# Chunk and residual loads issued from ScalarE's queue, and new lengths in a hand-written planner, in a convolution, attention and expert kernel

## The chip, the cores and the metric

The kernel runs on one core of a Trainium2 chip. A core has a matrix engine (TensorE, PE in the profile), a vector engine (VectorE, DVE), an activation engine (ScalarE, ACT), a general engine (GpSimd, POOL) and a queue engine (SyncE, SP) that issues transfers. Each works through its own list of instructions in order; semaphores order them between engines. The metric is the device time of one execution in microseconds (us); less is better.

## The reference

Input x is 8 images of 56 x 56 tokens with 128 channels, float32. In short:

```python
# layer 0: deformable convolution block
xp = x @ w_in + b_in
h = gelu(batchnorm(depthwise_conv3x3(x)))
offset = h @ w_off + b_off                    # 4 groups x 9 points x 2
mask = softmax(h @ w_msk + b_msk)             # over the 9 points
y = sum over points of mask * bilinear(xp, offset)
x = x + gamma1 * layer_norm(y @ w_out + b_out)
x = x + gamma2 * layer_norm(gelu(x @ w_fc1 + b_fc1) @ w_fc2 + b_fc2)
# layer 1: t = tokens of x, 3136 for each image
n = layer_norm(t)
t = t + softmax(causal((n @ Wq) @ (n @ Wk).T / sqrt(3136))) @ (n @ Wv)
n = layer_norm(t)
probs = softmax(n @ gate_w.T + gate_b, over the tokens)
# each of 64 experts takes its 8 best tokens of an image, pools them,
# runs gelu(. @ weight1) @ weight2, and adds the result back to them
t = t + scatter_add(...)
```

## The kernel before

All images go through one scheduled stage, then the experts' weights are streamed and the output is assembled (lines from 1050 on). An image is cut into 4 groups, three of 896 tokens and one of 448, so there are 32 groups. Seven generator functions each do one step for one group: `prepare` loads chunks of 448 tokens (xin), transposes them (ptx), copies them into a padded tile (xg), keeps a shifted copy for the residual (xc, stored to DRAM as xTd), and writes the projected image to DRAM (img). `plan` makes the 3x3 convolution (h), offsets and mask, and 25 tap weights a token (taps). `sample` gathers for each tile of 128 tokens 25 neighbours from DRAM (g, lines 471 to 496), multiplies them by the taps on VectorE (L484) and sums them on GpSimd (L489 to L496) into ys. `project` loads the residual (xT), transposes ys (pty), multiplies by w_out (py), normalises and adds (pta), runs the two layers (ph, hid, pm), normalises and adds again (ptb) and transposes back into t. `largest` makes the keys (zT), queries (qT) and the largest score of each query (sc, mx); `attend` makes scores again (st), exponentials (pe) and the weighted sum (av); `after` adds, normalises, makes the gate's logits (lg) and its best tokens (cv).

The groups are pipelined by a planner that runs when the kernel is built. Every generator yields `need(engine, us, ...)` ahead of each step: the engine that it takes, how long it is taken to last, whether it takes or gives one of the rotating PSUM buffers ("gen" 2, "sc" 3) or gather buffers ("g" 3), and from when its inputs are there (`since`). The planner keeps a time at which each engine is free and repeatedly advances the generator whose next step has the smallest start plus a lag for its place in the pipeline:

```python
min(able, key=lambda l: l.start() + BEHIND * (l.at + l.lag)).step()
```

The instructions are emitted in that order, so it fixes the order of every engine's list. The lengths only decide the order; at run time the semaphores decide the times. Nothing else hangs on the planner's times.

Loads are issued by SyncE in the order of emission. `bring` issues the load of a chunk, two chunks ahead; its tile has two buffers, so it waits until the transposes (L317) have read the chunk before the last one. `project` issues both residual loads of a group at its beginning (L557); that tile, too, has two buffers. The gathers (L479) are issued by SyncE, three to four transfers for a tile, and wait for one of three buffers. Stores of xTd, img, t2d and logd are issued by ScalarE.

Of the kernel before, what the change touches and what calls it, by code (L numbers as in the profile page):

```python
# [16 lines left out]
P = 128  # L17
C = 128
# [53 lines left out]
def local_kernel(ctx, tc, a, out, flag):  # L72
# [221 lines left out]

    xins = {}

    def bring(b, c, at):

        b, c = b + c // NCHUNK, c % NCHUNK
        if b < NB and (b, c) not in xins:  # L300
            xin = wk.tile([TP, 4, C], F32, tag="xin", name=f"xin{b}_{c}", bufs=2)
            nc.sync.dma_start(
                xin, x[b, c * CH : (c + 1) * CH, :].rearrange("(t p) d -> p t d", p=TP)
            )
            xins[b, c] = xin, at + 6.0

    def prepare(b, s):
        im = imgs[b % 2].rearrange("(h w) c -> h w c", w=IW)
        for c in range(2 * s, min(2 * s + 2, NCHUNK)):
            r = CHR * (c % 2)  # L310
            bring(b, c, 0.0)
            bring(b, c + 1, 0.0)
            xin, there = xins.pop((b, c))
            at = yield need(PE, 0.45, take="gen", since=there)
            pt = gen(f"ptx{b}_{c}")
            for i in range(4):
                nc.tensor.transpose(pt[:, i * TP : (i + 1) * TP], xin[:, i, :], ident[:TP, :TP])  # L317
            bring(b, c + 2, at)
            yield need(ACT, 2.0, give="gen")
            p3 = pt[:, :CH].rearrange("c (h w) -> c h w", w=HW)  # L320
            xg = rows_tile(b, s)
            nc.scalar.copy(xg[:, 1 + r : 1 + r + CHR, 1 : HW + 1], p3)
            xc = wk.tile([C, CH], F32, tag="xc", name=f"xc{b}_{c}")
            nc.scalar.activation(xc, pt[:, :CH], AF.Identity, bias=shift)
            nc.scalar.dma_start(xTd[b % 2][:, c * CH : (c + 1) * CH], xc)
            if r == 0 and c > 0:
                nc.scalar.copy(rows_tile(b, s - 1)[:, XROWS - 1, 1 : HW + 1], p3[:, 0])
            if r and c + 1 < NCHUNK:
                nc.scalar.copy(rows_tile(b, s + 1)[:, 0, 1 : HW + 1], p3[:, CHR - 1])
            yield need(PE, 0.95, take="gen")  # L330
            pq = gen(f"pq{b}_{c}")
            xf = xg.rearrange("c h w -> c (h w)")
            for i in range(4):

                f0 = (1 + r + 2 * i) * PW + 1
                nc.tensor.matmul(
                    pq[:W2, i * C : (i + 1) * C], xf[:, f0 : f0 + W2], w_in, start=True, stop=True
                )
            yield need(DVE, 0.7, give="gen")
            st = wk.tile([W2, 4, C], F32, tag="st", name=f"st{b}_{c}", bufs=2)  # L340
            nc.vector.tensor_add(
                st,
                pq[:W2, :].rearrange("p (t c) -> p t c", t=4),
                b_in.unsqueeze(1).to_broadcast([W2, 4, C]),
            )
            yield need(ACT, 0.8)
            for r in range(2):
                dst = im[2 + CHR * c + r : 2 + CHR * c + r + CHR - 1 : 2, 2 : HW + 2, :]
                nc.scalar.dma_start(dst.rearrange("t x c -> x t c"), st[r * PW : r * PW + HW])
# [4 lines left out]
    def plan(b, s):  # L354
# [3 lines left out]
        h = wk.tile([C, GT * P], F32, tag="h", name=f"h{b}_{s}")  # L358
        h3 = h[:, :N].rearrange("c (h w) -> c h w", w=HW)
        for k in range(NP):  # L360
            yield need(DVE, 0.15 + 0.0012 * N) if k else need(ACT, 0.2 + 0.001 * N)
            dy, dx = divmod(k, 3)
            src = xg[:, dy : dy + nr, dx : dx + HW]
            if k == 0:
                nc.scalar.activation(h3, src, AF.Copy, scale=dw[:, :1])  # L365
            else:
                nc.vector.scalar_tensor_tensor(  # L367
                    h3, src, dw[:, k : k + 1], h3, op0=ALU.mult, op1=ALU.add
                )
# [164 lines left out]
    def transposed(o, z, i0, m, n, name):  # L534
# [6 lines left out]
        yield need(ACT, 0.15 + 0.00085 * n, give="gen")  # L541
        nc.scalar.copy(o, pt[:, :n])

    def project(b, s):
        nm = f"{b}_{s}"
        nt, N = tiles(s), tokens(s)
# [2 lines left out]
        rest[b, s] = t  # L549
        if N < nt * P:  # L550
            nc.gpsimd.memset(t[:, nt - 1], 0.0)
        xTs = []
        for i0, m in banks(nt):
            n = min(m * P, N - i0 * P)
            r0 = (GT * s + i0) * P
            xT = wk.tile([C, 4 * P], F32, tag="xT", name=f"xT{nm}_{i0}", bufs=2)
            nc.sync.dma_start(xT[:, :n], xTd[b % 2][:, r0 : r0 + n])  # L557
            xTs.append(xT)
        for i0, m in banks(nt):
            n = min(m * P, N - i0 * P)  # L560
            xT = xTs.pop(0)
            yT = wk.tile([C, 4 * P], F32, tag="yT", name=f"yT{nm}_{i0}")
            if n < m * P:
                nc.gpsimd.memset(yT[:, n : m * P], 0.0)
            yield from transposed(yT[:, :n], ys, i0, m, n, f"y{nm}_{i0}")
            yield need(PE, 0.3 + 0.23 * m)
            py = ps.tile([P, 512], F32, tag="held", name=f"py{nm}_{i0}")
            nc.tensor.matmul(py[:, : m * C], three, b_out[:, : m * C], start=True, stop=False)
            for i in range(m):
                nc.tensor.matmul(  # L570
                    four(py, m)[:, i, :],
                    yT[:, i * P : (i + 1) * P],
                    w_out,
                    start=False,
                    stop=i == m - 1,
                )
            yield from add_normed(xT[:, :n], four(py, m), 0, f"a{nm}_{i0}")
            hid = wk.tile([P, 4, 4 * P], F32, tag="hid", name=f"hid{nm}_{i0}")
            if n < m * P:
                nc.gpsimd.memset(hid[:, :, n : m * P], 0.0)  # L580
            for f in range(4):
                there = yield need(PE, 0.0018 * n, take="gen", since=there if f else None)
                ph = gen(f"ph{nm}_{i0}_{f}")
                nc.tensor.matmul(  # L584
                    ph[:, :n], fc1[:, f * P : (f + 1) * P], xT[:, :n], start=True, stop=True
                )
                yield need(ACT, 0.15 + 0.00105 * n, give="gen", kind=GELU)
                nc.scalar.activation(  # L588
                    hid[:, f, :n], ph[:, :n], AF.Gelu, bias=b_fc1[:, f : f + 1]
                )  # L590
            yield need(PE, 0.3 + 0.92 * m)
            pm = ps.tile([P, 512], F32, tag="held", name=f"pm{nm}_{i0}")
            nc.tensor.matmul(pm[:, : m * C], three, b_fc2[:, : m * C], start=True, stop=False)
            for i in range(m):
                for f in range(4):
                    nc.tensor.matmul(  # L596
                        four(pm, m)[:, i, :],
                        hid[:, f, i * P : (i + 1) * P],
                        fc2[:, f, :],
                        start=False,  # L600
                        stop=i == m - 1 and f == 3,
                    )
            yield from add_normed(xT[:, :n], four(pm, m), 1, f"b{nm}_{i0}")

            yield need(PE, 0.12 * m, take="gen")
            pt = gen(f"pt2{nm}_{i0}")
            for i in range(m):
                w = min(P, n - i * P)
                nc.tensor.transpose(
                    pt[:w, i * C : (i + 1) * C], xT[:, i * P : i * P + w], ident  # L610
                )
            yield need(ACT, 0.6, give="gen")
            full = n // P
            nc.scalar.copy(t[:, i0 : i0 + full], four(pt, full))
            if full < m:
                nc.scalar.copy(t[: n % P, nt - 1], pt[: n % P, full * C : m * C])


    def moments(t, nt, name):
# [320 lines left out]
    free = {PE: 0.0, DVE: 0.0, ACT: 0.0, POOL: 0.0}  # L940
    rings = {"gen": [0.0] * 2, "sc": [0.0] * 3, "g": [0.0] * GB}
    table = [None]
    BEHIND = 1.0

    class Line:


        def __init__(self, make, lag, ready, source):
            self.make, self.ready, self.source, self.lag = make, ready, source, lag
            self.at, self.now, self.next, self.time, self.ended = 0, None, None, 0.0, {}  # L950

        def able(self):

# [7 lines left out]
                self.next = next(self.now)  # L961
            return not self.next.take or bool(rings[self.next.take])

        def start(self):
            n = self.next
            at = self.time if n.since is None else n.since
            if n.take:
                at = max(at, min(rings[n.take]) + (8.0 if n.take == "g" else 0.0))
            return max(at, free[n.engine])

        def step(self):
# [4 lines left out]
            if n.kind and n.kind != table[0]:  # L976
                table[0] = n.kind
                at += 1.3
            at += n.us
            free[n.engine] = at  # L980
            if n.give:
                rings[n.give].append(at)
            self.time = at + 0.1
            try:
                self.next = self.now.send(self.time)
            except StopIteration:
# [45 lines left out]
    while True:  # L1032
        able = [lines[o] for o in order if lines[o].able()]
        if not able:
            break
        min(able, key=lambda l: l.start() + BEHIND * (l.at + l.lag)).step()
    assert all(l.at == len(groups) for l in lines.values())


# [914 lines left out]
```

## Time and profile before

| | |
|---|---|
| median of 3 runs | 4209.79 us (4205.06 to 4210.52) |
| the profiled execution | 4213.55 us, its span 4211.7 us |
| TensorE's mean granted clock | 0.841 of full speed |
| DMA | 467.32 MB, mean 111 GB/s |
| SyncE's dynamic queue, q1 | 388.06 MB |
| ScalarE's dynamic queue, q10 | 74.60 MB |
| 0 to 3850 us: PE, DVE, ACT, POOL busy | 2914.50, 2513.91, 1676.36, 1946.31 us |
| 3850 to 4212 us: PE, DVE, ACT, POOL busy | 319.65, 75.51, 19.71, 1.24 us |

The span is the time from the first to the last instruction of the profiled execution; its device time is a little longer. Busy time of an engine counts what it computes, not the issuing of transfers and not its waits. "SPq" and "ACTq" are the queues in which SyncE and ScalarE wait and issue. A wait names the waiting engine, tile and line, then what it waited for: "PE ph L584 <- DVE xT L532" is TensorE waiting to start ph until VectorE has written xT. The chain of waits is followed back from the last instruction; it says which work the end hung on.

### The profile page before, as it was taken

What the parts mean: (1) busy time and instruction counts of PE and PEld (TensorE: products, weight loads), DVE (VectorE), ACT (ScalarE), POOL (GpSimd) and SP (SyncE); (2) the same over time, 40 slices, a digit from 0 to 9 for tenths busy, and PEclk for the clock granted to TensorE, in tenths of its full rate; (3) what the DMA queues carried; (4) which work ended last, traced back from release to release, by engine and by line L of the source; (5) the groups of instructions that cost most, each with busy time, mean ns of one, the idle gap of its engine ahead of it and who ended that gap; (6) DMA issues with size and microseconds to landing.
All of it is one profiled execution on the core that took longest, in us unless ns stands there. A gap on an engine that the chain in (4) does not pass through costs nothing.

```text
span 4211.7 us, 38352 instructions
## 1 busy us (share of the span) xinstructions
PE 3234.1 (77%) x12403; PEld 1980.6 (47%) x12403; DVE 2589.4 (61%) x4152; ACT 1696.1 (40%) x3738; POOL 1947.5 (46%) x1785
## 2 busy tenths in 40 slices
PE   3268589688875898588866988688848896996998
PEld 2134345344442444344443545444524453454987
DVE  5753676678665876577667776676757765531014
ACT  2133334444453544354453545444635453342000
POOL 1554555465445555554555545654565555201000
PEclk8578699889987999799987999899979997996555
DMA  5565444455444454544454455554454455003548
GB/s 150 113 131 112 98 112 109 102 118 121 99 100 104 106 111 96 122 107 111 100 122 95 108 110 111 119 115 107 105 121 103 109 112 113 15 11 103 155 135 247
DMA packets 333088, 467.32 MB, mean 111 GB/s; under 512 B 21080, under 2 KB 192908, under 8 KB 332364
## 3 DMA queue, kind: packets, MB, share of 16 engines
q1 hardware_dynamic: 209068, 388.06, 41.1%
q10 hardware_dynamic: 122784, 74.60, 6.6%
q0 software_dynamic: 1024, 2.10, 0.2%
q8 instruction: 100, 1.64, 0.2%
q14 instruction: 112, 0.92, 0.1%
HBM read 403.20 MB, written 61.49 MB: 110 GB/s over the span
## 4 chain that ended last, share of the span: by engine, by line
PE 36%; DVE 19%; POOL 11%; ACT 4%; issue 3%; DMA 3%; SPq 0%; DVEq 0%; ACTq 0%; POOLq 0%
PE sc L694 7%; DVE g L484 6%; PE av L778 6%; PE st L758 6%; POOL g L489 4%; PE epo L1097 3%; PE eph L1079 3%; POOL g L491 2%; PE ph L584 2%; DVE h L367 2%; PE pf L1130 2%; DVE taps L447 1%; PE pm L596 1%; DVE mx L709 1%; DMA g<-img 1%
## 5 line engine op out<-in xcount | busy, mean ns | idle before, releaser
L489 POOL TENSOR_TENSOR g<-g 128x1536 f32<-128x1536 f32 (+1 forms) x200 | 701.9, 3510 | 978.1 <-DVE g L484 874.2
L778 PE MATMUL av<-pe,zk 128*128 128x448 f32 (+6 forms) x1600 | 717.3, 539 | 92.7 <-ACT pe L771 82.3
L484 DVE TENSOR_TENSOR g<-g,tp 128x3200 f32<-128x3200 f32 (+1 forms) x200 | 694.7, 3478 | 44.8 <-ACT tp L467 16.8
L758 PE MATMUL st<-qT,zT 128*128 128x448 f32 (+6 forms) x1600 | 698.8, 527 | 3.8 <-ACT qT L729 1.3
L694 PE MATMUL sc<-zT,qT 128*128 128x512 f32 (+6 forms) x1600 | 650.7, 537 | 52.7 <-DVE mx L709 46.2
L709 DVE TENSOR_REDUCE mx<-sc 128x1 f32<-128x512 f32 (+6 forms) x800 | 451.3, 586 | 316.0 <-PE sc L694 268.2
L771 ACT ACTIVATE pe<-st 128x448 f32<-128x448 f32 (+6 forms) x800 | 393.5, 504 | 456.6 <-PE st L758 343.6
L778 PEld LDWEIGHTS av<-pe,zk 128*128 128x128 f32 (+1 forms) x1600 | 286.7, 200 | 317.6 <-issue 145.1
L694 PEld LDWEIGHTS sc<-zT,qT 128*128 128x128 f32 (+1 forms) x1600 | 283.7, 193 | 304.5 <-issue 130.1
L758 PEld LDWEIGHTS st<-qT,zT 128*128 128x128 f32 (+1 forms) x1600 | 300.1, 199 | 245.4 <-issue 217.7
L584 PE MATMUL ph<-xT,fc 128*128 128x512 f32 (+2 forms) x448 | 240.1, 654 | 200.6 <-DVE xT L532 178.6
L491 POOL TENSOR_TENSOR g<-g 128x768 f32<-128x768 f32 (+1 forms) x200 | 383.8, 1919 | 11.5
L367 DVE SCALAR_TENSOR_TENSOR h<-xg,dw,h 128x896 f32<-128x896 f32 (+1 forms) x256 | 356.4, 1392 | 7.4 <-ACT h L365 2.8
L584 PEld LDWEIGHTS ph<-xT,fc 128*128 128x128 f32 x448 | 91.8, 224 | 292.6 <-DVE xT L532 153.7
L596 PEld LDWEIGHTS pm<-fc,hid 128*128 128x128 f32 x1600 | 202.4, 196 | 44.3 <-issue 21.4
L596 PE MATMUL pm<-fc,hid 128*128 128x128 f32 x1600 | 214.2, 282 | 7.3 <-ACT hid L588 6.8
L493 POOL TENSOR_TENSOR g<-g 128x384 f32<-128x384 f32 (+1 forms) x200 | 212.6, 1063 | 13.3
L856 DVE MAX8 cv<-lg 64x8 f32<-64x896 f32 (+1 forms) x32 | 31.1, 972 | 278.4 <-ACT lg L843 278.4
L447 DVE TENSOR_TENSOR taps<-taps,a 128x252 f32<-128x252 f32 (+1 forms) x288 | 198.1, 688 | 1.3
L588 ACT ACTIVATE hid<-ph,b_fc 128x512 f32<-128x512 f32 (+2 forms) x224 | 138.8, 633 | 137.6 <-PE ph L584 136.0
L540 PE MATMUL pty<-ident,ys 128*128 128x128 f32 (+1 forms) x200 | 43.6, 324 | 176.9 <-POOL ys L496 171.0
L530 PE MATMUL ptb<-ident,ub 128*128 128x128 f32 (+1 forms) x200 | 50.4, 342 | 131.2 <-ACT ub L525 131.2
(238 smaller groups left out, 4979.0 us busy)
## 6 DMA issues: line engine op xcount, KB each, us to landing
g<-img SPq DMA_DIRECT2D x280, 700.0 KB
g<-img SPq DMA_DIRECT2D x56, 600.0 KB
g<-img SPq DMA_DIRECT2D x56, 500.0 KB
g<-img SPq DMA_DIRECT2D x56, 400.0 KB
g<-img SPq DMA_DIRECT2D x56, 300.0 KB
w2t<-in_L_ffn_weight_dram ACTq DMA_DIRECT2D x64, 256.0 KB
w1t<-in_L_ffn_weight_dram SPq DMA_DIRECT2D x32, 512.0 KB
xin<-in_x_dram SPq DMA_DIRECT2D x56, 224.0 KB
```

Source lines behind the costliest of these rows:

```text
L367: nc.vector.scalar_tensor_tensor(h3, src, dw[:, k : k + 1], h3, op0=ALU.mult, op1=ALU.add)
L447: nc.vector.tensor_add(dst, dst, a5[:, :nt, kx])
L484: nc.vector.tensor_mul(g3, g3, tp[:n, lt % 4].unsqueeze(2).to_broadcast([n, NTAP * NG, 32]))
L489: nc.gpsimd.tensor_add(g[:n, : 12 * C], g[:n, : 12 * C], g[:n, 12 * C : 24 * C])
L491: nc.gpsimd.tensor_add(g[:n, : 6 * C], g[:n, : 6 * C], g[:n, 6 * C : 12 * C])
L584: nc.tensor.matmul(ph[:, :n], fc1[:, f * P : (f + 1) * P], xT[:, :n], start=True, stop=True)
L596: nc.tensor.matmul(four(pm, m)[:, i, :], hid[:, f, i * P : (i + 1) * P], fc2[:, f, :], start=False, stop=i == m - 1 and f == 3,)
L694: nc.tensor.matmul(pp[:w, :n], qT[:, i * P : i * P + w], zTs[b, g][:, k0 : k0 + n], start=True, stop=not diagonal,)
L709: nc.vector.tensor_reduce(mx[:w, i, j : j + 1], pp[:w, :n], AX.X, ALU.max)
L758: nc.tensor.matmul(pp[:w, :n], zTs[b, g][:, j * P : j * P + w], qT[:, u * CH + q0 : (u + 1) * CH], start=True, stop=m <= 0,)
L771: nc.scalar.activation(pe[:w, :n], pp[:w, :n], AF.Exp, scale=SCALE)
L778: nc.tensor.matmul(av[:, q0:CH], zs[b, g][:w, j, :], pe[:w, : CH - q0], start=first, stop=last)
```

## The change

The chunk two ahead is loaded from ScalarE's queue, behind the copy that read the transposed chunk out of PSUM. The residual is loaded one bank at a time by `fetch`: from ScalarE's queue behind the copy of the bank two turns before, into the buffer that this bank has just left; the first ones, and any whose group is not yet prepared by then, from SyncE in `project`. The planner gets new lengths for the steps that now issue a load and for the convolution's taps; a factor on every length for each engine; 0.15 us between steps on different engines in place of 0.1 us behind every step; and, in the choice of the next step alone, 0.5 us more where the engine changes.

```diff
-    def bring(b, c, at):
+    def bring(b, c, at, queue):
 
         b, c = b + c // NCHUNK, c % NCHUNK
         if b < NB and (b, c) not in xins:
             xin = wk.tile([TP, 4, C], F32, tag="xin", name=f"xin{b}_{c}", bufs=2)
-            nc.sync.dma_start(
+            queue.dma_start(
                 xin, x[b, c * CH : (c + 1) * CH, :].rearrange("(t p) d -> p t d", p=TP)
             )
             xins[b, c] = xin, at + 6.0
...
-            bring(b, c, 0.0)
-            bring(b, c + 1, 0.0)
+            bring(b, c, 0.0, nc.sync)
+            bring(b, c + 1, 0.0, nc.sync)
             xin, there = xins.pop((b, c))
             at = yield need(PE, 0.45, take="gen", since=there)
             pt = gen(f"ptx{b}_{c}")
             for i in range(4):
                 nc.tensor.transpose(pt[:, i * TP : (i + 1) * TP], xin[:, i, :], ident[:TP, :TP])
-            bring(b, c + 2, at)
-            yield need(ACT, 2.0, give="gen")
+            yield need(ACT, 2.4, give="gen")
             p3 = pt[:, :CH].rearrange("c (h w) -> c h w", w=HW)
             xg = rows_tile(b, s)
             nc.scalar.copy(xg[:, 1 + r : 1 + r + CHR, 1 : HW + 1], p3)
+
+            bring(b, c + 2, at, nc.scalar)
             xc = wk.tile([C, CH], F32, tag="xc", name=f"xc{b}_{c}")
...
-            yield need(DVE, 0.15 + 0.0012 * N) if k else need(ACT, 0.2 + 0.001 * N)
+            yield need(DVE, 0.15 + 0.00139 * N) if k else need(ACT, 0.2 + 0.001 * N)
...
+    xTs = {}
+    turns = [(b, s, i0) for b in range(NB) for s in range(NGRP) for i0, _ in banks(tiles(s))]
+
+    def fetch(b, s, i0, queue):
+
+        if (b, s, i0) in xTs or not done("prepare", NGRP * b + s):
+            return
+        n = min(4 * P, tokens(s) - i0 * P)
+        r0 = (GT * s + i0) * P
+        xT = wk.tile([C, 4 * P], F32, tag="xT", name=f"xT{b}_{s}_{i0}", bufs=2)
+        queue.dma_start(xT[:, :n], xTd[b % 2][:, r0 : r0 + n])
+        xTs[b, s, i0] = xT
...
-        xTs = []
         for i0, m in banks(nt):
             n = min(m * P, N - i0 * P)
-            r0 = (GT * s + i0) * P
-            xT = wk.tile([C, 4 * P], F32, tag="xT", name=f"xT{nm}_{i0}", bufs=2)
-            nc.sync.dma_start(xT[:, :n], xTd[b % 2][:, r0 : r0 + n])
-            xTs.append(xT)
-        for i0, m in banks(nt):
-            n = min(m * P, N - i0 * P)
-            xT = xTs.pop(0)
+            fetch(b, s, i0, nc.sync)
+            xT = xTs.pop((b, s, i0))
...
-            yield need(ACT, 0.6, give="gen")
+            yield need(ACT, 1.0, give="gen")
             full = n // P
             nc.scalar.copy(t[:, i0 : i0 + full], four(pt, full))
             if full < m:
                 nc.scalar.copy(t[: n % P, nt - 1], pt[: n % P, full * C : m * C])
+
+            here = turns.index((b, s, i0)) + 2
+            if here < len(turns):
+                fetch(*turns[here], nc.scalar)
...
-    BEHIND = 1.0
+    BEHIND, SLACK = 1.0, 0.5
+    LONGER = {PE: 1.1, DVE: 1.05, ACT: 1.05, POOL: 1.05}
...
-        def start(self):
+        def start(self, slack=0.0):
             n = self.next
             at = self.time if n.since is None else n.since
+            if n.engine != self.last:
+                at += 0.15 + slack
             if n.take:
                 at = max(at, min(rings[n.take]) + (8.0 if n.take == "g" else 0.0))
             return max(at, free[n.engine])
...
-            at += n.us
+            at += n.us * LONGER[n.engine]
             free[n.engine] = at
             if n.give:
                 rings[n.give].append(at)
-            self.time = at + 0.1
+            self.time, self.last = at, n.engine
...
-        min(able, key=lambda l: l.start() + BEHIND * (l.at + l.lag)).step()
+        min(able, key=lambda l: l.start(SLACK) + BEHIND * (l.at + l.lag)).step()
```

More of the change, by code (lines that the diff above doesn't have):

```diff
@@ L949, in __init__ @@
             self.make, self.ready, self.source, self.lag = make, ready, source, lag
-            self.at, self.now, self.next, self.time, self.ended = 0, None, None, 0.0, {}
+            self.at, self.now, self.next, self.ended = 0, None, None, {}
+            self.time, self.last = 0.0, None
         def able(self):
```

## The prediction

> **What bounds the kernel now.** I read the page first: busy times, then the chain.
>
> ```profile
> span 4211.7 us, 38352 instructions
> ...
> PE 3234.1 (77%) x12403; PEld 1980.6 (47%) x12403; DVE 2589.4 (61%) x4152; ACT 1696.1 (40%) x3738; POOL 1947.5 (46%) x1785
> ...
> PE 36%; DVE 19%; POOL 11%; ACT 4%; issue 3%; DMA 3%; SPq 0%; DVEq 0%; ACTq 0%; POOLq 0%
> ```
>
> No engine is full. The chain in order of time starts at 964 us, so its shares add up to 77%, not 100%. Of what it covers, TensorE has 47%, VectorE 25%, GpSimd 14%, ScalarE 5%, transfers 4%. The work passes from engine to engine, and the time is set by how well the four in-order programs fit each other. The windows say where: 0 to 3850 us is the scheduled stage (TensorE busy 2914.50 us, VectorE 2513.91, ScalarE 1676.36, GpSimd 1946.31). The expert stage after it is untouched by the change.
>
> Next, the waits of SyncE's own queue, which issues this stage's loads (gx apart):
>
> ```profile
> SPq L479 <- POOL ys L496: 917.0, 115, 14.4
> ...
> SPq L302 <- PE ptx L317: 389.2, 22, 39.7
> SPq L479 <- DMA xTd<-xc: 274.3, 33, 17.8
> ```
>
> The columns are total us, times, longest. The first is the ordinary wait for a gather buffer. The second is a chunk load that stands at the head of the queue until TensorE has read the buffer's old chunk; gathers (L479) stand behind it. The third is a gather waiting for an older ScalarE transfer to complete.
>
> What the engines lose by that is small. In the waits of all engines, those for a transfer are far down, and those between engines lead:
>
> ```profile
> POOL g L489 <- DVE g L484: 874.2, 140, 19.4
> ...
> PE ph L584 <- DVE xT L532: 178.6, 14, 36.0
> ...
> PE pty L540 <- POOL ys L496: 171.0, 21, 15.6
> ...
> POOL g L489 <- DMA g<-img: 27.5, 5, 7.1
> ```
>
> TensorE's two waits there average 12.8 and 8.1 us, far over what one operation lasts: it arrives where the planner put it, and the other engine is late. The chain holds pieces of all three loads concerned (start, us, what):
>
> ```profile
> 1260.83 8.08 DMA xin<-in_x_dram
> ...
> 1512.74 10.24 DMA g<-img
> ...
> 2259.59 4.16 DMA xT<-xTd
> ```
>
> **Part one: SyncE's queue is freed.** By the instruction order of the two programs, 54 of 56 chunk loads and 54 of 56 residual loads go to ScalarE's queue. The chunk load is issued behind ScalarE's copy xg, which had to wait for the transposes that read the old chunk; so the wait of 389.2 us has nothing left to wait for. The residual load is issued two turns ahead, behind the copy t that waited for the buffer's last transposes. Gain: the chain's long pieces are 9.41 + 10.24 + 6.51 + 3.86 + 6.39 + 7.40 = 43.8 us of gathers, 8.1 of xin, 4.2 of xT, together 56.1 us between 964 and 3600. Scaled to a stage of 3600 us, x 3600/2636 = 77 us. That is the upper end; the lower is 0, since gathers still wait 917.0 us for GpSimd and 274.3 us and more for ScalarE's transfers. I take half, **-38 us**, because only the gathers that stood behind a chunk load gain. Where this stall goes, GpSimd's ys is late next.
>
> The Trainium skill speaks against a gain here: "DMA: Bandwidth & Descriptors", section "Issuing engines are not separate DMA queues", has transfers of all engines on the same 16 DMA engines, so that another issuing engine saves issue time alone. By it the term would be about 0; the wait of 389.2 us is issue time of that kind, and the trace decides for it.
>
> **Part two: ScalarE's new work.** The issues last 0.323 us (xin, median) and 0.368 us (xT): 54 x 0.323 + 54 x 0.368 = 37 us on ScalarE. Behind each xin issue stand xc, its store and the edge copies; behind each xT issue stands usually the next exponential pe, for which TensorE's av waits. ScalarE is idle for over half of the stage, so the lower end is its share of the chain, 5% or 2 us; the upper is 37. I take a quarter, **+9**. What waits come with them: 106 of the 108 also wait for the completion counter of an earlier transfer, often a gather. The nearest rows are ScalarE's waits for transfers before: 5.4 + 2.5 + 1.9 + 0.8 + 0.6 = 11.2 us for the 240 transfers it issues in this stage, 0.047 us each, so 5 us for 108. The far end is what SyncE pays when the other queue is late, 274.3/33 = 8.3 us each. I take **+5**, because the same engine and the same counters gave the first row; the far end becomes a rival.
>
> **Part three: the order.** This is the larger part, and it has no row of its own. Nearly every position on every engine changes. Four things can be counted.
>
> Planned against measured lengths: the lengths written into the steps before add up to 2541 us on TensorE, 2290 on VectorE, 1829 on GpSimd. In the trace these took 2914, 2514, 1946 up to 3850 us, so the plan has 0.87, 0.91, 0.94 of them. With the new lengths and factors it has 2541 x 1.1 = 2795, 2328 x 1.05 = 2444, 1829 x 1.05 = 1920, that is 0.96, 0.97, 0.99. TensorE was 4% short against VectorE and 7% against GpSimd; it is now 1% and 3% short. ScalarE was too long in the plan and stays so. Also, steps that change engines are preferred 0.5 us later, which gives producers time. The gain is bounded by TensorE's two late-partner waits, 178.6 + 171.0 = 349.6 us: at most half of it (175), and at worst none. I take a fifth, **-70**, since sums cannot say that each place improves.
>
> Table loads: the scheduled stage has 272 loads of ScalarE's function table before and 298 after (gelu against exp changes more often). Each lasts 1.283 us:
>
> ```profile
> 2439.80 1.28 ACT L771 ACT_TABLE_LOAD   x1
> 2441.09 0.98 ACT L771 ACTIVATE pe<-st 128x448 f32<-128x448 f32 x2
> 2442.09 1.28 ACT L588 ACT_TABLE_LOAD   x1
> 2443.38 0.69 ACT L588 ACTIVATE hid<-ph,b_fc 128x512 f32<-128x512 f32 x1
> ```
>
> 26 x 1.283 = 33 us; the next function starts 0.01 us behind a load, so nothing is added. ScalarE's share of the chain makes it 2, all of it 33; a quarter gives **+8**. The Trainium skill ("ScalarE: Activation LUTs", "What ACT_TABLE_LOAD costs") has a drain with each switch, about 2.66 us in all, which would make it 69 instead of 33; the rows above show no such drain.
>
> TensorE back to back: between py and its pta ScalarE squares (4 x 0.47), GpSimd takes the root (0.20 + 1.02) and ScalarE scales once (0.37), 3.5 us; with four hand-overs of 0.1 us (VectorE's multiply ended at 2222.21 us and GpSimd's add began at 2222.29) 3.9 us. In the order before, 5 of 56 py are followed at once by their pta, in the order after 21. That is 16 x 3.9 = 62 us if TensorE had other work, 0 if it had not (the planner puts nothing between where nothing is ready). A fifth: **+12**.
>
> **Small edits.** The gather's multiply, taps, attention and all arithmetic are the same and keep their durations. The xc copy starts 0.32 us later, behind the xin issue, and its store waits that much; TensorE's pq needs xg alone. Both are in part two.
>
> **Sum.** -38 + 9 + 5 - 70 + 8 + 12 = -74 us. The profiled execution took 4213.55 us (span 4211.7 and 1.85 outside), and the median of the runs is 3.76 us lower, 4209.79. 4213.55 - 74 - 3.76 = 4135.8; I forecast **4136 us**, 1.8% less.
>
> **Rivals.**
>
> *ScalarE is held by the counters* (slower). Its loads wait for gathers that SyncE can't issue yet because GpSimd hasn't freed a buffer; behind them stand pe, hid and tp, and TensorE's av waits. Against it: ScalarE lost 11.2 us on 240 such transfers. For it: SyncE lost 8.3 us at each of 33. Nine such holds (75 us) cancel the forecast's gain; one transfer in eight, 13.5 x 8.3 = 112, gives 4136 + 112 = 4248 us.
>
> *The order is worse on TensorE* (slower). The project chain stands back to back 16 times more, and no late partner comes earlier: the 70 is lost, the 12 becomes 62. 4136 + 70 + 50 = 4256 us. It decides if TensorE's waits for ua and sqa grow by more than its waits for xT and ys shrink.
>
> *The freed queue buys nothing*, since the chunk loads' place is taken by waits for ScalarE's transfers (the row of 274.3 us, grown): 4136 + 38 = 4174 us, still faster.
>
> *The order cancels out*: no late partner comes earlier, and the rest nearly cancels, 4136 + 70 = 4206 us, no change.
>
> **How the numbers follow.** A measurement of this kernel can tell about 0.2% (8 us) from no change. Chances: forecast 0.51, queue buys nothing 0.13, order cancels 0.07, ScalarE held 0.15, order worse 0.14. So faster 0.64, same 0.07, slower 0.29. The low end takes part one whole (77), a third of TensorE's late-partner waits (117), and the costs at 2 + 5 + 2 + 0: 4209.79 - 77 - 117 + 9 = 4025. The high end, 4255, takes in the held ScalarE and reaches the worse order; beyond it and below the low end I leave some 2 in 10. The two faster cases by themselves span 4025 to 4200.
>
> **What the profile after would show.** Part one is right if SyncE's wait at the chunk load is gone and its waits for ScalarE's transfers haven't grown by as much; wrong if gathers land as late as before. Part two is right if ScalarE's waits for transfers stay under 20 us. Part three is right if TensorE's waits of ph for xT and pty for ys fall together by 70 us or more, VectorE's waits for lg and pq with them, and wrong if ua, sqa or pe take their place. Table loads should number 298 in this stage. The forecast is wrong if TensorE's busy time to the end of the stage is the same and the stage doesn't end some 70 us sooner.

## The result, and the profile after

| | before | after |
|---|---|---|
| median | 4209.69 us (4205.06 to 4210.52) | 4376.91 us (4367.02 to 4379.38) |
| ratio to before | 1 | 1.0395 [1.0377, 1.0413] |
| span of the profiled execution | 4211.7 us | 4375.6 us |
| TensorE busy, and the rest of the span | 3234.1 and 977.6 us | 3292.7 and 1082.9 us |
| TensorE's mean granted clock | 0.841 | 0.834 |
| the last gather multiply starts at | 3615.4 us | 3782.7 us |

The kernel became 4.0% slower; the forecast was 1.8% faster, and the time lies above the whole range. The loss is in the scheduled stage: the last multiply of the gathers is 167.3 us later, and the span is 163.9 us longer. Of those, TensorE idles 105.3 us more and is busy 58.6 us more with the same 12403 matmuls.

The page of the changed kernel, with the chain's shares:

```profile
span 4375.6 us, 38323 instructions
...
PE 3292.7 (75%) x12403; PEld 1984.1 (45%) x12403; DVE 2576.0 (59%) x4152; ACT 1730.1 (40%) x3764; POOL 1921.2 (44%) x1785
...
PE 38%; DVE 19%; POOL 17%; ACT 4%; issue 3%; DMA 2%; SPq 0%; DVEq 0%; POOLq 0%; ACTq 0%
```

GpSimd's share of the chain went from 11 to 17%, though it does the same work. The waits of all engines say why (total us, times, longest):

```profile
POOL g L490 <- DVE g L485: 1047.0, 155, 14.7
...
PE pty L541 <- POOL ys L497: 423.1, 60, 20.3
DVE xT L533 <- PE pta L531: 367.7, 43, 21.5
...
PE ph L592 <- DVE xT L533: 30.9, 20, 9.0
...
DVE g L485 <- DMA g<-img: 12.3, 2, 11.8
```

Two of the same rows before:

```profile
DVE xT L532 <- PE pta L530: 47.5, 12, 20.8
...
DVE g L484 <- DMA g<-img: 14.1, 2, 12.0
```

GpSimd waits for VectorE's multiply g (874.2 before), TensorE for GpSimd's sums ys (171.0 before), VectorE for TensorE's pta (47.5 before). That is one ring: g, ys, pty, py, pta, xT, each late for the next. Of the ring's waits only that of ph for xT fell, from 178.6. And the last line matters most: VectorE waited for gathers to land for 12.3 us in all, against 14.1 before. Taken from the landings in the trace, a tile's last transfer was there 29.9 us before its multiply began (median of 200 tiles; 25.1 before). The gathers are not late. The multiply is.

SyncE's own waits show what the change took away and what came:

```profile
SPq L480 <- POOL ys L497: 1146.6, 145, 12.8
...
SPq L480 <- DMA img<-st: 286.8, 39, 24.4
SPq L480 <- DMA t2d<-t: 285.0, 19, 29.0
SPq L480 <- DMA xin<-in_x_dram: 264.7, 25, 26.3
...
SPq L480 <- DMA xT<-xTd: 142.8, 21, 10.3
```

The 389.2 us at the chunk load are gone. Gathers now wait 407.5 us for the chunk and residual loads on ScalarE's queue; before, when SyncE issued these loads itself, that was 2.6 us. It looks like the rival "the freed queue buys nothing", only dearer. The experiments show that it isn't.

A stretch of the changed kernel shows the multiply being late. First VectorE (start us, duration, instruction, in square brackets the idle time before it):

```profile
2098.34 0.62 DVE L533 SCALAR_TENSOR_TENSOR xT<-pta,c_L_conv_ln_g,xT 128x384 f32<-128x384 f32 x1 [0.41 <-PE pta L531]
...
2103.86 0.68 DVE L368 SCALAR_TENSOR_TENSOR h<-xg,dw,h 128x448 f32<-128x448 f32 x1
...
2104.99 3.47 DVE L485 TENSOR_TENSOR g<-g,tp 128x3200 f32<-128x3200 f32 x1
```

Then GpSimd in the same stretch:

```profile
2096.09 0.91 POOL L510 TENSOR_TENSOR ssa<-ssa,half 128x3 f32<-128x3 f32 x1
2108.53 3.55 POOL L490 TENSOR_TENSOR g<-g 128x1536 f32<-128x1536 f32 x1 [11.53 <-DVE g L485]
```

From 2098.34 us on, VectorE does other work without a break (normalisation, masks, weights, the convolution's h) and reaches the multiply at 2104.99, while GpSimd stands idle for 11.53 us. By the trace, the tile's transfers had all landed by 2071.8 us, and its weights tp were begun at 2036.2. Nothing holds the multiply but its place in VectorE's list.

### The profile page after: what moved, and what is told of

It reads as the page before. It is cut to its first block, busy times and chain, and to the rows that moved or that the text cites. A ratio compares the mean times of both kernels' runs of the same rounds, so it can differ in the third digit from the quotient of the medians.

```text
span 4375.6 us, 38323 instructions
## 1 busy us (share of the span) xinstructions
PE 3292.7 (75%) x12403; PEld 1984.1 (45%) x12403; DVE 2576.0 (59%) x4152; ACT 1730.1 (40%) x3764; POOL 1921.2 (44%) x1785
## 4 chain that ended last, share of the span: by engine, by line
PE 38%; DVE 19%; POOL 17%; ACT 4%; issue 3%; DMA 2%; SPq 0%; DVEq 0%; POOLq 0%; ACTq 0%
PE sc L706 7%; DVE g L485 7%; PE st L770 6%; PE av L790 6%; POOL g L490 6%; POOL g L492 3%; PE ph L592 3%; PE epo L1113 3%; PE eph L1095 3%; PE pm L604 2%; DVE h L368 2%; POOL g L494 2%; DVE mx L721 2%; PE pf L1146 1%; DVE taps L448 1%
## 5 line engine op out<-in xcount | busy, mean ns | idle before, releaser
L706 PE MATMUL sc<-zT,qT 128*128 128x512 f32 (+6 forms) x1600 | 682.7, 544 | 46.1 <-DVE mx L721 45.7
L485 DVE TENSOR_TENSOR g<-g,tp 128x3200 f32<-128x3200 f32 (+1 forms) x200 | 695.3, 3478 | 13.7 <-DMA g<-img 12.3
L541 PE MATMUL pty<-ident,ys 128*128 128x128 f32 (+1 forms) x200 | 54.1, 338 | 440.2 <-POOL ys L497 423.1
L368 DVE SCALAR_TENSOR_TENSOR h<-xg,dw,h 128x896 f32<-128x896 f32 (+1 forms) x256 | 358.2, 1399 | 10.5 <-ACT h L366 7.0
L533 DVE SCALAR_TENSOR_TENSOR xT<-pta,c_L_conv_ln_g,xT 128x512 f32<-128x512 f32 (+2 forms) x56 | 38.2, 682 | 367.7 <-PE pta L531 367.7
L541 PEld LDWEIGHTS pty<-ident,ys 128*128 128x128 f32 (+1 forms) x200 | 29.3, 159 | 487.4 <-POOL ys L497 455.4
L604 PE MATMUL pm<-fc,hid 128*128 128x128 f32 x1600 | 204.7, 278 | 2.4 <-ACT hid L596 2.3
```

Of the source, the lines that this page charges most:

```text
L368: nc.vector.scalar_tensor_tensor(h3, src, dw[:, k : k + 1], h3, op0=ALU.mult, op1=ALU.add)
L485: nc.vector.tensor_mul(g3, g3, tp[:n, lt % 4].unsqueeze(2).to_broadcast([n, NTAP * NG, 32]))
L604: nc.tensor.matmul(four(pm, m)[:, i, :], hid[:, f, i * P : (i + 1) * P], fc2[:, f, :], start=False, stop=i == m - 1 and f == 3,)
L706: nc.tensor.matmul(pp[:w, :n], qT[:, i * P : i * P + w], zTs[b, g][:, k0 : k0 + n], start=True, stop=not diagonal,)
```

## The experiments

Two theories stood at first: the loss is in the new order (theory 1 of the texts), or in the loads (theory 2); theory 3 has both. All ratios are to the kernel before.

**The two halves.** One kernel has the new loads with the old planner (SLACK 0, factors 1, old lengths, 0.1 us behind every step); one has the old loads with the new planner and lengths.

```diff
 # loads_only, against after
-    BEHIND, SLACK = 1.0, 0.5
-    LONGER = {PE: 1.1, DVE: 1.05, ACT: 1.05, POOL: 1.05}
+    BEHIND, SLACK = 1.0, 0.0
+    LONGER = {PE: 1.0, DVE: 1.0, ACT: 1.0, POOL: 1.0}
...
 # order_only, against after
-            bring(b, c + 2, at, nc.scalar)
+            bring(b, c + 2, at)
...
-                fetch(*turns[here], nc.scalar)
```

Expected of loads_only: 

> The changed loads (chunk and residual from ScalarE's queue), with the planner and all lengths as before. Theory 1, the order: the 167 us come from the new planner, so this kernel stands at 4210 us or up to 38 us below it, TensorE's waits of pty for ys stay near 171 us. Theory 2, the loads: gathers wait for ScalarE's transfers (in the changed kernel 264.7 us for xin and 142.8 us for xT), so this kernel loses most of the 167 us: 4320 us or more. Theory 3, both halves need each other: somewhere between, 4250 to 4300 us.

Expected of order_only: 

> The loads as before from SyncE's queue, with the new planner and all its new lengths. Theory 1, the order: 4340 us or more, pty waiting over 350 us for ys. Theory 2, the loads: 4250 us or less, pty waiting under 250 us. Theory 3: between them, and the two parts' losses don't add up to 167 us.

Measured: loads_only 4393.22 us, 1.0436 [1.0418, 1.0453]; order_only 4112.56 us, 0.9765 [0.9748, 0.9781]. TensorE's wait for ys, with the loads alone:

```profile
PE pty L541 <- POOL ys L497: 504.8, 66, 35.5
```

and with the order alone:

```profile
PE pty L540 <- POOL ys L496: 181.6, 24, 20.3
```

The loads cost 183 us on the old order and 264 on the new one; the order by itself gains 97. Both times lie where theory 2 put them. Theory 1 falls.

**Parts of the order, with the loads in.** `SLACK = 0.0` in one, all four factors 1.0 in the other.

Expected of no_slack: 

> The changed kernel with the 0.5 us in the choice of the next step set to 0; factors, lengths and the 0.15 us between engines stay. If that preference makes the order bad (it puts steps of the line that stays on its engine first, and TensorE's project chain too close behind GpSimd): 4250 us or less and pty's wait for ys back under 250 us. If the lengths and factors make it bad: 4340 us or more.

Expected of no_factors: 

> The changed kernel with the factors 1.1 and 1.05 set to 1; the 0.5 us preference and the lengths stay. If the factors make the order bad (TensorE's plan is stretched 5% more than the others', so its steps are put in a place where GpSimd isn't ready): 4250 us or less. If the preference does: 4340 us or more, like the changed kernel.

Measured: no_slack 4436.32 us, 1.0551 [1.0533, 1.0569], so the slack was worth 59 us; no_factors 4336.07 us, 1.0302 [1.0285, 1.0319], so the factors cost 41. Neither comes near the 264, and what follows shows that such numbers hold only for the lists that the build made of them.

**The queue or the place.** The loads moved in two senses: to ScalarE's queue, and to another place in the program. All four kernels have the new planner.

```diff
 # sp_place: both at the new place, from SyncE; xin_sp and xT_sp: one of the two
-            bring(b, c + 2, at, nc.scalar)
+            bring(b, c + 2, at, nc.sync)
...
-                fetch(*turns[here], nc.scalar)
+                fetch(*turns[here], nc.sync)
 # queue_only, against order_only: both at the old place, from ScalarE
-            nc.sync.dma_start(xT[:, :n], xTd[b % 2][:, r0 : r0 + n])
+            nc.scalar.dma_start(xT[:, :n], xTd[b % 2][:, r0 : r0 + n])
...
```

Expected of sp_place: 

> The changed kernel with both loads where the change puts them (chunk behind the copy xg, residual two turns ahead behind the copy t), but issued from SyncE instead of ScalarE; planner and lengths of the changed kernel. Theory Q, the queue: what costs is that the gathers on SyncE wait for completion counters that loads on ScalarE hold until ScalarE comes to them. Then this kernel is near the one with the change's order alone, 4113 us, and within 4080 to 4170; SyncE's gathers wait for no chunk or residual load. Theory P, the place: what costs is where the loads stand in the emission, since the build then moves the gather's multiply, GpSimd's sums and pty later on their engines. Then it stays near the changed kernel's 4377 us, 4300 to 4400, and TensorE's wait of pty for ys stays over 350 us (182 with the order alone).

Expected of queue_only: 

> The opposite corner: planner and lengths of the changed kernel, both loads at their old places in the program (chunk behind the transposes, residuals at the beginning of project), but all of them issued from ScalarE. Theory Q: over 4300 us, and SyncE's gathers wait some 400 us for chunk and residual loads. Theory P: near 4113 us, at most 4170. If both count, both corners lie between, and their distances from 4113 us add up to some 264 us.

Expected of xin_sp: 

> The changed kernel with the chunk load alone back on SyncE, at its new place; the residual load stays on ScalarE. Theory Q with the price shared as SyncE's waits are in the changed kernel (264.7 us for chunk loads, 142.8 for residuals, so 65 to 35): 4113 + 0.35 x 264 = 4205 us. Theory P: 4377 us, within 70.

Expected of xT_sp: 

> The changed kernel with the residual load alone back on SyncE, at its new place; the chunk load stays on ScalarE. Theory Q, shared in the same way: 4113 + 0.65 x 264 = 4285 us. Theory P: 4377 us, within 70.

| new planner | loads from SyncE | loads from ScalarE |
|---|---|---|
| old place | 4112.56 | 4365.36, 1.0372 [1.0354, 1.0389] |
| new place | 4189.31, 0.9953 [0.9936, 0.9970] | 4376.91 |

With the chunk load alone on SyncE the time is 4280.73 us, 1.0168 [1.0151, 1.0185]; with the residual load alone on SyncE 4212.95, 1.0011 [1.0001, 1.0020]. The queue costs 188 to 253 us, the place 12 to 77: theory Q by size, though sp_place lies 19 us above its range. But its mechanism already fails here. The shares by SyncE's waits were the wrong way round: the residual load alone on ScalarE costs 91 us over sp_place, the chunk load alone 24 (both together 188), where SyncE's waits had them 35 to 65. And VectorE's wait for gathers doesn't follow the cost: 10.5 us in sp_place, 9.3 in xin_sp, 14.2 in xT_sp, 12.3 in after, in queue_only there is no such row, and order_only, the fastest of these, has the most, 52.8. Something other than late gathers follows from the queue.

**The order kept.** The instruction order of the built programs gave the next theory. What the planner emits isn't what each engine gets: the build, which makes the engines' lists from the emitted program, moves instructions past each other. A place is one instruction in an engine's list. Counted in the traces, by setting each list beside that of the same planner with the emitted order kept, loads_only has the multiply g on average 20.0 places later on VectorE than before; against order_only it is 23.0 places later in after and 23.4 in queue_only, but 14.3 to 15.5 in the other three. (The texts below give about a third of these for g on VectorE; their places for ys on GpSimd and for h agree with the traces within 2.) The next kernels keep the planner's order on the four computing engines; SyncE's list stays the build's.

```diff
-    while True:
-        able = [lines[o] for o in order if lines[o].able()]
+    En = mybir.EngineType
+    with tc.manual_schedule(engines={En.PE, En.DVE, En.Activation, En.Pool}):
+        while True:
+            able = [lines[o] for o in order if lines[o].able()]
...
 # after_dve: engines={En.DVE, En.Pool}
```

Expected of order_only_man: 

> The change's order alone (loads from SyncE at their old places, new lengths), with the scheduled stage's instructions on TensorE, VectorE, ScalarE and GpSimd kept in the order in which the planner emits them; SyncE's list is left to the build. Without this the build moves instructions on: the gather's multiply g stands on average 16 places later on VectorE than emitted, ys 11 places later on GpSimd. It is the base of the next kernel. Both theories leave its level open, 3950 to 4200 us; the estimate is 4080, some 30 us under the 4113 us without the fixed order, since g and ys come earlier and 24 of TensorE's waits for ys took 182 us.

Expected of after_man: 

> The changed kernel with the order on the same four engines kept as emitted; every computing instruction then has the same place as in the kernel above, and only the 108 loads stand elsewhere, on ScalarE. Theory R, the build's re-placement: the 264 us came from the places that the build gave to g, ys and pty once loads on ScalarE shared the completion counters; then this kernel is within 40 us of the one above, and TensorE's waits for ys agree within 60 us. Theory C, the counters at run time: gathers wait on the chip for ScalarE's loads and everything behind is late; then it is 200 us or more above it, and SyncE's waits for chunk and residual loads stay near 400 us.

Expected of after_dve: 

> The changed kernel with the emitted order kept on VectorE and GpSimd alone; TensorE, ScalarE and SyncE are left to the build. Theory R with its place on VectorE and GpSimd (g and ys): within 60 us of the changed kernel with all four engines kept, and far under 4377. If the place of pty, pta or tp on TensorE and ScalarE carries the loss, it stays above 4300. Theory C: above 4300 too.

Expected of before_man: 

> The kernel before with the emitted order kept on the four engines: old lengths, loads from SyncE. If the gain of the new lengths (95 us with the build's re-placement) is the planner's own, this kernel is 70 to 120 us above the order-only kernel with the emitted order kept, so some 4175 us by the estimate of 4080; if the gain came from how the build re-placed the two, they are within 30 us of each other.

| | as built | order kept | ratio, order kept | g later on VectorE as built, places |
|---|---|---|---|---|
| before | 4209.69 | 3916.83 | 0.9306 [0.9291, 0.9322] | 51.7 |
| order_only | 4112.56 | 3944.49 | 0.9365 [0.9349, 0.9380] | 48.2 |
| after | 4376.91 | 3900.70 | 0.9262 [0.9247, 0.9278] | 71.2 |

after_dve, with the lists of VectorE and GpSimd alone kept, took 3912.41 us, 0.9296 [0.9280, 0.9311]. The page of after_man:

```profile
span 3897.1 us, 38304 instructions
...
PE 3202.4 (82%) x12403; PEld 1920.0 (49%) x12403; DVE 2620.7 (67%) x4152; ACT 1709.7 (44%) x3742; POOL 1972.9 (51%) x1785
```

its waits:

```profile
PE pty L541 <- POOL ys L497: 16.3, 2, 15.1
...
DVE g L485 <- DMA g<-img: 9.2, 3, 5.5
```

and those of order_only_man, whose computing instructions stand in the same order:

```profile
DVE g L484 <- DMA g<-img: 50.4, 9, 9.3
...
PE pty L540 <- POOL ys L496: 16.3, 2, 15.1
```

TensorE's waits for ys fall from 423.1 us to 16.3 in after, at an unchanged program text of every step. Theory R holds: the 264 us are not in the loads. Its "within 40 us" was still a little wrong, and on the other side: after_man is 43.8 us *faster* than order_only_man. Theory C falls. The estimate of 4080 for the level was far off: keeping the order is worth 168 to 476 us in these three. And the new lengths, worth 97 us as built, cost 28 us in the order that they were made for: within the 30 that the text on before_man gave to the build's re-placing, and of the other sign than the planner's own gain.

**Which list, and what in it.** The changed kernel with VectorE's list alone kept (`engines={En.DVE}`), and with GpSimd's alone (`engines={En.Pool}`).

Expected of after_v: 

> The changed kernel with the emitted order kept on VectorE alone. If the place of the gather's multiply on VectorE carries the 264 us (it then stands on average 23.5 places earlier than in the changed kernel, and the build puts GpSimd's sums 8.5 places earlier by itself): at most 4000 us, with TensorE's waits of pty for ys under 60 us. If GpSimd's list carries it: over 4250.

Expected of after_p: 

> The changed kernel with the emitted order kept on GpSimd alone. The gather's multiply then stands 18.1 places earlier on VectorE, the sums 13.7 places earlier on GpSimd, by the build's own following. If only VectorE's own order matters, the time is nearer to 4377 than to 3912; if what matters is that the multiply comes early, by whichever list, it is under 4050 us.

Measured: after_v 3965.43 us, 0.9418 [0.9403, 0.9434]; after_p 4305.96 us, 1.0231 [1.0214, 1.0249]. Keeping VectorE's list alone gains 411 of the 476 us, with TensorE's waits for ys at 18.2 us; keeping GpSimd's alone gains 71. TensorE's waits in after_p:

```profile
PE ptb L531 <- ACT ub L526: 279.7, 42, 23.3
PE pta L531 <- ACT ua L526: 233.1, 34, 24.3
...
PE pty L541 <- POOL ys L497: 46.3, 4, 20.0
```

With GpSimd's list kept and VectorE's left to the build, the wait for ys goes, but it returns as waits for ua and ub. Their roots (ssa, ssb) are GpSimd's too and stand behind sums that wait 1151.7 us for VectorE's g. Keeping GpSimd's list alone moves the wait along.

The last two kernels leave VectorE's list to the build but for one thing. In after_g nothing that was emitted behind a multiply may be put ahead of it; in after_h only the convolution's taps h keep their place.

```diff
 # after_g, behind the planner's loop (muls: names of the multiplies)
...
+    held = None
+    edge = mybir.DependencyInfo(mybir.DependencyClass.NoSync, mybir.DependencyReason.DATA)
+    for ins in nc.cur_bb.bb.instructions:
+        if ins.engine == mybir.EngineType.DVE:
+            if held:
+                tc.add_manual_dep(ins, held, edge, reason="behind the multiply")
+            if ins.name in muls:
+                held = ins.name
...
 # after_h
-                nc.vector.scalar_tensor_tensor(
+                tc.keep_in_program_order(nc.vector.scalar_tensor_tensor(
...
```

Expected of after_g: 

> The changed kernel, where on VectorE nothing that was emitted behind a gather's multiply g may be put ahead of it; all else on VectorE and everything on the other engines is left to the build. If being overtaken is what makes g late and that is the whole loss on VectorE: within 60 us of the 3965 us with VectorE's whole order kept. If the order of the other VectorE work counts as much, over 4100 us.

Expected of after_h: 

> The changed kernel, where on VectorE only the convolution's taps h (264 instructions that the build puts on average 31 places ahead) keep their place behind what was emitted before them; g still stands 17.6 places later than emitted instead of 23.5. If it is h that overtakes g and costs the time: under 4150 us. If any overtaking work does: over 4200 us, and TensorE's waits of pty for ys stay over 250 us.

Measured: after_g 3980.64 us, 0.9458 [0.9442, 0.9474]; after_h 4299.90 us, 1.0216 [1.0199, 1.0233]. TensorE's wait for ys and VectorE's for gathers in after_g:

```profile
DVE g L485 <- DMA g<-img: 16.0, 8, 3.6
PE pty L542 <- POOL ys L498: 14.6, 1, 14.6
```

and TensorE's wait in after_h:

```profile
PE pty L541 <- POOL ys L497: 281.1, 41, 17.7
```

Forbidding any work to overtake the multiply gains 396 of the 476 us; holding h alone gains 77. And with the multiplies no longer behind their emitted places (by the trace 3.1 ahead on average) VectorE waits only 16.0 us for gathers: the data was there. But after_g doesn't single out the multiply. Its edit also holds the rest of VectorE's list closer to the emitted order: the other instructions, counted among themselves, stand 3.7 places from it on average, against 8.7 in after. For the multiply speaks that they stand 8.4 places off in order_only too, which is 264 us faster and has the multiply 23.0 places less late. Against it speaks after_p: there the multiply is only 16.3 places late and the others stand 9.8 off, and the time is 4306 us. That VectorE's list carries the loss is shown; how much of it is the multiply's own place is not.

**What the loads do when the lists stay.** The loads at the new place from SyncE, order kept (sp_place_man), and the loads with the old planner, order kept (loads_only_man).

Expected of sp_place_man: 

> Loads at the change's places, issued from SyncE, new lengths, order kept on the four engines; the computing instructions have the same places as in the two kernels at 3944 (old place, SyncE) and 3901 us (new place, ScalarE). If ScalarE's queue brings the 44 us: 3944 within 12. If the place does, since the loads then have nothing to wait for at the head of SyncE's queue: 3901 within 12, and SyncE's wait of the chunk load for the transposes, 904.8 us with the old place, is mostly gone.

Expected of loads_only_man: 

> Old lengths and planner, loads from ScalarE at the change's places, order kept on the four engines; the computing instructions stand as in the kernel before with kept order (3917 us). If the parts add up: 3917 - 44 = 3873 us, the fastest so far. VectorE's wait for gathers to land was 45.8 us there and should fall under 15; if it falls by as much and the time by less than 15 us, the gain is taken up by another wait.

Measured: sp_place_man 3953.76 us, 0.9396 [0.9380, 0.9411]; loads_only_man 3891.62 us, 0.9245 [0.9230, 0.9261]. SyncE's waits with both loads on it, at the new place:

```profile
SPq L302 <- PE ptx L317: 805.3, 50, 31.4
...
SPq L555 <- DVE xT L533: 630.3, 54, 28.2
```

The place buys nothing: 9 us more than order_only_man, within the 12 that the text allowed. On SyncE, whose list is the build's, the chunk loads stand among the gathers where they stood in order_only_man (within one transfer), the residual loads on average 2.2 transfers earlier, and both wait much as there (904.8 us at the chunk load, 451.6 at the residual). The queue buys 53 us. It is seen where the gathers arrive: VectorE's wait for them is 68.5 us in sp_place_man, 50.4 in order_only_man and 9.2 in after_man. The parts don't add up fully: loads_only_man was expected at 3873, and the loads gain 25 us there instead of 44, the lengths lose 9, which is not clear of the noise, instead of 28 with the loads in. VectorE's wait for gathers fell from 45.8 to 6.8, that is by 39, so some 14 us were taken up elsewhere; where wasn't tried.

loads_only_man is the fastest version: the change's loads, the old lengths, and the order kept, 7.5% under the kernel before. after_man is 9 us behind it, and their intervals overlap.

## Why the prediction was wrong, point by point

**The step that failed is one that the sum took for granted**: that the order of emission "fixes the order of every engine's list", as the description of the kernel has it. It doesn't. In the kernel before, the multiply g already stood 51.7 places later than emitted. The prediction saw that "nearly every position on every engine changes" and put all of it down to the planner; with the planner unchanged, 20.0 places at g and 183 us came from the loads alone. No term and no rival had that, so the range had no room for it.

**Part one** (-38, between 0 and 77) was right in mechanism and near in size where the lists stay: the loads gain 43.8 us with the new lengths and 25 with the old ones, through gathers that land earlier, as forecast. As built they cost 183 to 264. The sign was lost to the lists, not to the queue. By its first sign it would have been right as built: the 389.2 us at the chunk load are gone, and SyncE's waits for ScalarE's transfers in the stage grew by less, from 901.0 to 1177.2 us. Yet the loads made the kernel slower; SyncE's waits don't tell what the engines lose. Its other sign, "wrong if gathers land as late as before", didn't decide it either, because in the kernel as built VectorE hardly waited for gathers at all: 14.1 us before. The 56.1 us of transfers on the chain were no measure of what earlier gathers can bring there.

The rule quoted against it, from the Trainium skill ("DMA: Bandwidth & Descriptors", "Issuing engines are not separate DMA queues"), allows another issuing engine only the issue time, usually small. Here the queue alone brought 53 us (sp_place_man against after_man), since what it saves is not the issuing but the waiting at the head of SyncE's list (805.3 us at the chunk load, 630.3 at the residual); the measurement decides.

**Part two.** ScalarE's waits for transfers in the stage came to about 41 us (9.9 + 9.3 + 5.8 + 4.5 and smaller ones) instead of 16, over the 20 that were named as the limit. The counters' price was too low, but it isn't the loss: after_man has the same loads on ScalarE, 42.9 us of such waits, and gains. The issues' 9 us weren't isolated.

**Part three** (-70) looks confirmed by order_only's -97 and isn't. TensorE's two late-partner waits, which should fall together by 70, fell from 349.6 to 280.2 us there, 69.4, so even the test that the prediction set was all but passed; in after as built they rose to 454.0. VectorE's waits for lg and pq, which should fall with them, did fall in after, from 403.8 to 202.0 us, and the kernel was slower all the same. But with the order kept the same lengths cost 28 us. The gain came from what the build made of the new lists. The two small terms can't be checked by themselves: 298 table loads were forecast and 298 came, and TensorE's wait of pta for ua rose by 31.7 us, from 70.8 to 102.5, as the back-to-back count warned, between its 12 and its 62.

**The rivals.** ScalarE was not held by the counters (41 us, 112 needed). "The order is worse on TensorE" is met by its own sign: the wait for ua grew by 31.7 us, and those for ys and xT didn't shrink, they grew together by 104.4. But it put this down to the planner, and order_only, with the same planner, is faster than the kernel before. "The freed queue buys nothing" had the right row, grown to 407.5 us of waits for the two loads, and the wrong consequence: these waits of SyncE cost little in themselves, as SyncE also waited 1146.6 us for buffers to come free. In after_man the two rows are 95.4 and 55.5 us, and the time is the best but one.

**What stays open** is why the build puts the multiply further back when the loads are on ScalarE. The transfers of both queues share completion counters: in the trace of after, eight semaphores take 153 or 154 transfers each, 50 to 63 of them ScalarE's. So by the build's own reckoning gathers may come later than they do; that was argued from the programs and not shown. That the mean place of g isn't the whole measure is shown: it stands 16.3 places late in after_p and 53.1 in after_h, and both take 4300 us; in sp_place and xin_sp it stands 63.6 places late, and they are 91 us apart.

## What to carry to other kernels

Before a change is costed by the order in which a program is written, compare that order with the list that each engine really gets; an edit that only moves loads can move the computing past itself. When a consumer (GpSimd, TensorE) waits for an engine that is neither idle nor waiting for data, look at what stands ahead of the missing instruction in that engine's list: here, keeping other work from being put ahead of one multiply was worth 396 us. And test a new order, a length or a queue with the lists held still, or each measurement is of the lists that it happened to cause.

## What the runs showed that was not expected

TensorE's granted clock was higher where TensorE was fed more closely. It was 0.834 in after (0.826 to 0.835 over its four runs), 0.885 in after_man (0.877 to 0.886) and 0.889 in loads_only_man, and TensorE's busy time fell from 3292.7 us in after to 3202.4 in after_man for the same matmuls: of the 478.5 us between the spans of after and after_man, 90.3 are busy time and 388.2 idle time. In the 500 us from 500 us on it was busy for 392.59 us at a clock of 0.86 in after, and for 428.30 us at 0.94 in after_man. The Trainium skill ("TensorE: Matmul & The Clock Gate", "Part 1: The HAM clock gate (the "warmup" mystery)") has the clock set by how busy the engine has recently been, with which these rows agree in direction; the forecast had no term for it. That the waiting lowered the clock, and not something else, wasn't tried by itself.

A wait can also be large and cost little: the gathers of after_man stood in SyncE's list for 2128.4 us until sums or multiplies had ended (1232.4 and 896.0), and VectorE waited for a gather to land for 9.2 us.
